# A graph layer on one core: 107 picked sets and 985 gathered chunks in place of 109 and 945, with the spare rows gathered a turn later

## The chip, the cores and the metric

The kernel runs on one core of a Trainium2 chip. A core has a matrix engine (PE), a vector engine (DVE), a scalar engine (ACT), a general engine (POOL, also called GpSimd), a queue engine (SP), and 16 DMA engines that move data between the chip's main memory and the core's own memory. Each engine works through its own list of instructions in order, and waits on semaphores where it needs another's result.

The metric is the device time of one execution in microseconds (us). The kernel before took 1822.46 us as the median of three runs (1816.8, 1824.37, 1822.46). One more execution was recorded by the profiler; it took 1817.15 us, and its span of instructions is 1815.4 us.

## The reference

```python
# x: (12500, 128) f32; src, dst: (400000,) int32, sorted by dst; edge_type: 0 or 1
Xs = X[src]
m_data = Xs @ W_data.T + b_data
m_ctrl = Xs @ W_control.T + b_control
msg = jnp.where((edge_types == 0)[:, None], m_data, m_ctrl)
agg = jax.ops.segment_sum(msg, dst, num_segments=X.shape[0])
out = jax.nn.relu(agg + (X @ W_self.T + b_self))
return layernorm(X + out)
```

For every edge the row of its source node is taken, sent through one of two matrices, and summed over the edges of each destination node. The kernel sums the rows of x by destination and type first, and multiplies by the matrices after that, 25 times for 500 nodes each.

## The kernel before

**Chunks, groups, sets.** The 400000 edges, sorted by destination, are 3125 chunks of 128 edges. 125 chunks are a group (25 groups, about 500 destination nodes each). A group is five stretches of 25 chunks, each of 5 chunks of one kind ("p", gathered) and 20 of the other ("e", picked). The rows of x of a chunk can reach PE in two ways:

- **Gathered**: one indirect DMA on POOL's queue reads the 128 rows of a chunk (three bf16 parts of each, 768 bytes, 96 KB in all) from a table in main memory into a tile `msg` (`fetch`, line 742). PE then sums them by destination with three matmuls and a fourth that counts (`gathered`, `chunk`, line 773), the columns chosen by a 0/1 matrix `psel` that DVE makes for five or 25 chunks at once.
- **Picked**: the 20 chunks of one stretch are a *set*. All of x lies in the core's memory as 98 blocks of 128 rows. The edges of a set are sorted into cells by block, at most 32 to a cell, and a 0/1 matrix `pick` lets PE pull their rows out of the blocks: 96 to 98 matmuls a set into `got`, copied by ACT into `emsg` (12 copies), then 75 matmuls with `esel`, and 25 that count. DVE makes `O`, `prod`, `rm`, `rv`, `pick` and `esel` for it, some 27 instructions. `there` and `pick` go through main memory on SP's queue (6.2 KB out, 800 KB back).

Some cells get more than 32 edges. What is too much, up to 64 rows of a set, are the **spare rows**: their list `idx` is made by PE and ACT (`spare_slots`, `keep`), and one more indirect DMA on POOL's queue reads them into a tile `last` (`spare_rows`, line 789). ACT fills the other half of `last` (`last_rows`, line 827, the copy at L831), and PE reads it with the last three matmuls of the set (`sums<-esel,last`).

**How many sets a group has.** `sets(g)` (line 176) gives 5 for every third group, else 4. Where it is 4, the last stretch of the group is gathered as a whole, 25 chunks (`of_p`, line 180). With g from 0 to 24, nine groups have five sets and 16 have four: 109 sets, and 945 gathered chunks.

**The order of the work.** The loop at line 1058 runs over the 109 sets. A set has six *turns* of four blocks (`unit(t)`, line 845, t from 0 to 5), and `merged` sorts what else is to be done between them: the gathered chunks, spread evenly over the sets from the third on; the making of the matrices for the sets to come; the preparation of the next group's codes; and, where a group's last chunk has passed, its finishing (`finish`, `pass_on`, `begin_acc`). The end of a set (`end`, line 877) is issued behind the first matmuls of the next one (`ending()` in turn 0). In it `keep_codes` also makes the `idx` of the next set on ACT.

**The order on POOL's queue.** `paced` (line 752) is called twice a turn. Each call issues at most one gather, and ties it to a matmul of that turn (`gate`), so that it can't start before. If a spare gather is asked for it goes first; else the next chunk's gather, if it is due: its due time is the place of the chunk 14 before it (`AHEAD`, line 1053). In the second call of an even turn only a chunk that was due two and a half turns earlier is taken. 18 tiles `msg` exist (`HOLD`). The spare gather is asked for in turn 1 (lines 847 and 848), and from turn 2 on the tile `last` stands for the last block (line 861 ff). In a steady set of nine chunks the gathers are thus issued in the turns 0, 1 (spare), 1, 2, 2 or 3, 3, 4, 5, 5 or the like.

Of the kernel before, what the change touches and what calls it, by code (L numbers as in the profile page):

```python
# [29 lines left out]
NE = 5  # L30
# [116 lines left out]
def evenly(units, a=0.0, b=1.0):  # L147
    return [(a + (b - a) * (k + 0.5) / len(units), u) for k, u in enumerate(units)]


def short_path(ctx, tc, const, ident, eps, wT, brow, bad, x, src, dst, etype, ws, bs, out):
# [12 lines left out]
    def side():  # L164

        return ps1.tile([P, 512], FP, name="side")
# [8 lines left out]

    def sets(g):

        return NE if g % 3 == 0 else NE - 1

    def of_p(g, i):  # L180

        return PL if sets(g) < NE and i == NE - 1 else PB
# [3 lines left out]

    rows_p = (NE - 1) * PB + PL
    each_e = [(g, i) for g in range(NG) for i in range(sets(g))]
    raw = {}
    starts = {k: [c for kind, _, c, _ in windows(0) if kind == k] for k in "pe"}  # L190
# [309 lines left out]
    def select(sel, col, code2):  # L500

        rows, n, width = sel.shape
        shape = [rows, n, width // 2, 2]
        nc.vector.tensor_tensor(  # L504
            sel.rearrange("p n (w t) -> p n w t", t=2),
            col[:rows].rearrange("p (o w t) -> p o w t", o=1, t=2).to_broadcast(shape),
            code2.rearrange("p n (o t) -> p n o t", o=1).to_broadcast(shape),
            op=OP.is_equal,
        )
        return sel  # L510
# [179 lines left out]
    def sums():  # L690
        return ps2.tile([P, 512], FP, name="sums")

    def cells_of(ps, width, k):
        return ps[:, k * 2 * width:(k + 1) * 2 * width]

    def add_rows(out, msg, sel, start, stop):
        for j in range(3):
            nc.tensor.matmul(  # L698
                out, msg[:, j * D:(j + 1) * D], sel, start=(start and j == 0), stop=stop, skip_group_check=True
            )  # L700
# [21 lines left out]
    def pass_on(g):  # L722

        assert parts_in[g] == NE + sets(g)
        if g + 1 < NG:
            begin_acc(g + 1)
            added.append(nc.vector.tensor_add(acc[g + 1][:, :, :lap], acc[g + 1][:, :, :lap], acc[g][:, :, GN:]))

    def accumulate(g, i, ps, wide, width):

        begin_acc(g)
        parts_in[g] = parts_in.get(g, 0) + 1
        with tc.issue_after(added[-2].ins) if len(added) > 1 else ExitStack():
            at = nc.vector.value_load(raw["place"][0:1, g, i:i + 1], min_val=0, max_val=R - WMAX)
        win = acc[g][:, :, bass.ds(at, width)]
        added.append(nc.vector.tensor_add(win, win, ps[:, :4 * wide].rearrange("p (a w) -> p a w", w=wide)[:, :, :width]))  # L736
# [15 lines left out]
    def paced(now, gate):  # L752

        if spare:
            gather = spare.pop()()
        elif to_fetch and due[len(due) - len(to_fetch)] <= now:
            gather = fetch()
        else:
            return
        tc.add_manual_dep(  # L760
            gather.ins, gate.ins.name,
            mybir.DependencyInfo(mybir.DependencyClass.Sync, mybir.DependencyReason.DATA), reason="paced",
        )
# [25 lines left out]
    def spare_rows(w):  # L789
        msg = slots[w]["last"] = two.tile([P, 3 * D], BF, name="last")  # L790
        return nc.gpsimd.indirect_dma_start(  # L791
            out=msg[:OVF, :], out_offset=None, in_=rows3[:, :],
            in_offset=bass.IndirectOffsetOnAxis(ap=slots[w]["idx"], axis=0),
        )

    def picked(w, tiled, ending, fin_used, before):

        g, i = each_e[w]  # L800
        s = {"sel": {}, "msg": {}}
        per, pair = 4, 2

        def choose(q0, n=8):

            sel = select(sp.tile([P, 9, 2 * EW], BF, name="esel")[:, :n], code_col, slots[w]["code"][:, q0:q0 + n])
            for k in range(n):
                s["sel"][q0 + k] = sel[:, k]

        def pick(ps, q, a0=0):  # L810
            for a in range(a0, 4):
                last = nc.tensor.matmul(  # L812
                    ps[CAP * a:CAP * (a + 1), :], slots[w]["pick"][:, a * NQ + q, :],
                    x3[:, 4 * q + a - a0].rearrange("p j d -> p (j d)"), start=True, stop=True, skip_group_check=True,
                )
            return last

        def rows(q):
            ps = psg.tile([P, pair, 512], FP, name="got")
            msg = two.tile([P, pair, 3 * D], BF, name="emsg", bufs=5)  # L820
            for k in range(pair):
                last = pick(ps[:, k, :3 * D], q + k)
                s["msg"][q + k] = msg[:, k, :]
            nc.scalar.copy(msg, ps[:, :, :3 * D])  # L824
            return last

        def last_rows():
            q = NQ - 1
            ps = psg.tile([P, pair, 512], FP, name="got")[:, 0] if fin_used else side()
            pick(ps[:, :3 * D], q, 2)  # L830
            nc.scalar.copy(s["msg"][q][OVF:, :], ps[OVF:, :3 * D])  # L831

        def count(q):
            if q == 0:
                s["ps"] = sums()
            nc.tensor.matmul(  # L836
                cells_of(s["ps"], EW, 1)[CAP * (q % 4):CAP * (q % 4 + 1), :], one_col[:, :CAP], s["sel"][q],
                start=(q < 4), stop=(q + 4 >= NQ), skip_group_check=True,
            )

        def add(q0, q1):
            for q in range(q0, q1):
                add_rows(cells_of(s["ps"], EW, 0), s["msg"].pop(q), s["sel"][q], False, q == NQ - 1)

        def unit(t):

            if t == 1 and w > 0:
                spare.append(lambda: spare_rows(w))
            for q in range(t * per, (t + 1) * per, pair):
                gate = rows(q)  # L850
            paced(w + (t + 1) / turns, gate)
            if t % 2:
                paced(w + (t + 1) / turns, gate)
            else:
                paced(w + (t - 1.5) / turns, gate)
            if t in (0, 1):
                choose(8 * t)
            if t == 0:
                ending()
            if t == 2:  # L860
                assert not spare
                s["msg"][NQ - 1] = slots[w]["last"]
            if t == 3:
                choose(16, 9)
            if t > 0:
                for q in range((t - 1) * per, t * per if t < turns - 1 else NQ):
                    count(q)
            if t == turns - 2:
                last_rows()
            if t == 1 and before:  # L870
                before()
            if t > 0:
                add((t - 1) * per, t * per)
            for u in tiled.get(t, []):
                u()

        def end():

            early, *more = tiled.get(turns, [lambda: None])
            early()  # L880
            add((turns - 1) * per, NQ)
            for u in more:
                u()
            accumulate(g, 2 * i + 1, s["ps"], EW, EW)

        turns = (NQ - 1) // per
        return evenly([lambda t=t: unit(t) for t in range(turns)]), end


# [165 lines left out]
    def ending():  # L1055
        pass

    for w in range(pairs):
        g, i = each_e[w]
# [181 lines left out]
```

## Time and profile before

| | |
|---|---|
| median of three runs | 1822.46 us (1816.8 to 1824.37) |
| the profiled execution | 1817.15 us, span 1815.4 us |
| TensorE clock granted | 0.995 of full speed |
| gathers on POOL | 945 of chunks, 109 of spare rows |
| set, from L831 to L831 | 15.92 us on the mean of 108 |
| main memory traffic | 236.28 MB read, 18.01 MB written |

How to read the lines of the profile. PE is the matmuls, PEld the loading of their weights beside them. A group of instructions is given as: line, engine, operation, written tile `<-` read tiles, shapes, `x` count, then busy us and mean ns of one, and behind the second bar the idle time of that engine just before them, with what ended most of it. A row of the timeline begins with the start and the duration in us, and has in brackets the idle time before it and what released it. A row of waits names who waited, for whom, the total in us, the number of times and the longest. "issue" is idle time in which the engine waited for nothing that the profile shows. A row of one tile's or one line's instructions gives the least, median and greatest duration in ns and the first and last start in us. A row of a window gives its start and end, its length, the busy time of the engine and (x) the number of instructions, the granted clock, the share of the DMA engines and GB/s.

### The profile page before, as it was taken

What the parts mean: (1) busy time and instruction counts of PE and PEld (TensorE: products, weight loads), DVE (VectorE), ACT (ScalarE), POOL (GpSimd) and SP (SyncE); (2) the same over time, 40 slices, a digit from 0 to 9 for tenths busy, and PEclk for the clock granted to TensorE, in tenths of its full rate; (3) what the DMA queues carried; (4) which work ended last, traced back from release to release, by engine and by line L of the source; (5) the groups of instructions that cost most, each with busy time, mean ns of one, the idle gap of its engine ahead of it and who ended that gap; (6) DMA issues with size and microseconds to landing.
All of it is one profiled execution on the core that took longest, in us unless ns stands there. A gap on an engine that the chain in (4) does not pass through costs nothing.

```text
span 1815.4 us, 72710 instructions
## 1 busy us (share of the span) xinstructions
PE 1637.4 (90%) x30253; PEld 1300.4 (72%) x30253; DVE 1600.0 (88%) x4050; ACT 1265.9 (70%) x2501; POOL 1328.1 (73%) x1071
## 2 busy tenths in 40 slices
PE   0589899998999999999999999999999999999997
PEld 0367677777777777777777777777777777777776
DVE  8889999998988998999898989898898988898883
ACT  4567667776777677676777767676776777777675
POOL 0387878887787778777776888778777777777772
PEclk9999999999999999999999999999999999999999
DMA  8744453554455453453545444544434444444431
GB/s 228 221 145 144 126 160 115 161 153 138 127 160 159 119 159 100 155 157 120 157 122 172 135 149 120 156 155 119 151 110 153 149 150 124 140 157 130 140 117 55
DMA packets 189216, 259.13 MB, mean 143 GB/s; under 512 B 86081, under 2 KB 154987, under 8 KB 185804
## 3 DMA queue, kind: packets, MB, share of 16 engines
q1 hardware_dynamic: 127402, 149.67, 25.3%
q0 software_dynamic: 48848, 98.32, 19.6%
q10 hardware_dynamic: 12626, 6.40, 1.3%
q8 instruction: 238, 3.90, 0.9%
q14 instruction: 102, 0.84, 0.1%
HBM read 236.28 MB, written 18.01 MB: 140 GB/s over the span
## 4 chain that ended last, share of the span: by engine, by line
PE 33%; DVE 23%; DMA 10%; ACT 4%; issue 3%; DVEq 1%; SPq 0%; ACTq 0%
PE sums L698 15%; PE got L812 10%; DMA pick<-there 8%; DVE esel L504 4%; PE side L942 2%; DVE pick L684 2%; ACT emsg L824 2%; DVE rv L630 2%; PE side L642 2%; DVE found L602 2%; DVE prod L571 2%; DMA there<-cell 1%; PE sums L836 1%; DVE rm L504 1%; ACT h L972 1%
## 5 line engine op out<-in xcount | busy, mean ns | idle before, releaser
L747 POOL DMA_INDIRECT msg<-rows,pidx x945 | 1191.0, 1260 | 320.7 <-issue 190.6
L824 ACT CAST emsg<-got 128x768 bf16<-128x768 f32 x1308 | 983.1, 802 | 259.7 <-PE got L812 246.7
L698 PE MATMUL sums<-esel,emsg 128*128 128x176 bf16 x7848 | 718.8, 241 | 0.0
L698 PEld LDWEIGHTS <-emsg 128*128 128x128 bf16 x7848 | 571.4, 98 | 110.1 <-issue 91.8
L812 PE MATMUL got<-x,pick 128*32 128x384 bf16 x10512 | 572.0, 330 | 35.0 <-ACT emsg L824 29.1
L812 PEld LDWEIGHTS <-pick 128*32 128x32 bf16 x10682 | 237.1, 96 | 152.7 <-issue 42.1
L504 DVE TENSOR_TENSOR esel<-code_col,code 128x1408 bf16<-128x1408 bf16 x327 | 297.6, 910 | 9.5 <-PE sums L698 6.8
L791 POOL DMA_INDIRECT last<-rows,idx x109 | 133.4, 1224 | 140.8 <-ACT emsg L824 119.7
L698 PE MATMUL sums<-psel,msg 128*128 128x48 bf16 x2835 | 186.7, 184 | 1.6 <-DVE psel L504 1.6
L836 PE MATMUL sums<-esel,one_col 128*32 128x176 bf16 x2725 | 156.3, 240 | 18.2 <-DVE esel L504 16.9
L684 DVE TENSOR_SCALAR pick<-pick,lane_f 128x3200 bf16<-128x3200 bf16 x109 | 115.0, 1055 | 51.5 <-DMA pick<-there 51.1
L698 PEld LDWEIGHTS <-msg 128*128 128x128 bf16 x2835 | 152.5, 97 | 2.4 <-issue 2.2
L783 PE MATMUL sums<-psel,one_col 128*128 128x48 bf16 x945 | 150.7, 183 | 0.0
L736 DVE TENSOR_TENSOR acc<-acc,sums 128x352 f32 (+2 forms) x234 | 100.6, 430 | 52.4 <-PE sums L698 44.6
L504 DVE TENSOR_TENSOR O<-cell_col,blk 128x2000 bf16<-128x2000 bf16 x109 | 129.9, 1191 | 6.5 <-PE side L642 2.4
L593 DVE TENSOR_TENSOR prod<-O,ahead 128x2000 bf16<-128x2000 bf16 x109 | 129.7, 1190 | 0.0
L836 PEld LDWEIGHTS <-one_col 128*32 128x32 bf16 x2725 | 80.4, 97 | 59.3 <-issue 24.9
L642 PE MATMUL side<-rv,O 128*128 128x64 bf16 x2180 | 85.9, 196 | 39.4 <-DVE rv L630 39.0
L642 PEld LDWEIGHTS <-O 128*128 128x128 bf16 x2180 | 78.9, 101 | 45.8 <-DVE rv L630 44.0
L624 ACT CAST bits_b<-bits 128x24 bf16<-128x24 int32 x109 | 23.2, 213 | 117.6 <-DVE bits L622 111.3
L783 PEld LDWEIGHTS <-one_col 128*128 128x128 bf16 x945 | 90.5, 96 | 0.0
L630 DVE TENSOR_TENSOR rv<-rm,vals 128x1280 bf16<-128x1280 bf16 x109 | 89.0, 816 | 0.0
(172 smaller groups left out, 1959.7 us busy)
## 6 DMA issues: line engine op xcount, KB each, us to landing
pick<-there SPq DMA_DIRECT2D x109, 800.0 KB
acc<-acc_start SPq DMA_DIRECT2D x23, 1280.0 KB
msg<-rows,pidx POOLq DMA_INDIRECT x945
rows<-x SPq DMA_DIRECT2D x6, 1344.0 KB
xs<-in_x_dram SPq DMA_DIRECT2D x99, 62.5 KB
out_dram<-h SPq DMA_DIRECT2D x99, 62.5 KB
xt<-in_x_dram ACTq DMA_DIRECT2D x6, 896.0 KB
there<-cell SPq DMA_DIRECT2D x109, 6.2 KB
```

The costliest lines, as they stand in the source:

```text
L504: nc.vector.tensor_tensor(sel.rearrange("p n (w t) -> p n w t", t=2), col[:rows].rearrange("p (o w t) -> p o w t", o=1, t=2).to_broadcast( ...
L593: nc.vector.tensor_tensor(prod, s["O"], ahead.rearrange("p (o j) -> p o j", o=1).to_broadcast([P, EC, NCELL]), op=OP.mult)
L630: nc.vector.tensor_tensor(rv.rearrange("p c v (r t) -> p c v r t", t=2), rm.rearrange("p c (o r t) -> p c o r t", o=1, t=2).to_broadcast(s ...
L642: nc.tensor.matmul(s["rk"][:m, :2 * CAP], s["held"][:, c * NCELL:c * NCELL + m], s["rv"][:, c].rearrange("p v r -> p (v r)"), start=(c == ...
L684: nc.vector.tensor_scalar(t, t, lane_f, None, op0=OP.is_equal)
L698: nc.tensor.matmul(out, msg[:, j * D:(j + 1) * D], sel, start=(start and j == 0), stop=stop, skip_group_check=True)
L747: return nc.gpsimd.indirect_dma_start(out=msg, out_offset=None, in_=rows3[:, :], in_offset=bass.IndirectOffsetOnAxis(ap=codes["p", g][0][: ...
L783: nc.tensor.matmul(cnt, one_col, sel, start=False, stop=(c == n - 1), skip_group_check=True)
L791: return nc.gpsimd.indirect_dma_start(out=msg[:OVF, :], out_offset=None, in_=rows3[:, :], in_offset=bass.IndirectOffsetOnAxis(ap=slots[w][ ...
L812: last = nc.tensor.matmul(ps[CAP * a:CAP * (a + 1), :], slots[w]["pick"][:, a * NQ + q, :], x3[:, 4 * q + a - a0].rearrange("p j d -> p (j ...
L824: nc.scalar.copy(msg, ps[:, :, :3 * D])
L836: nc.tensor.matmul(cells_of(s["ps"], EW, 1)[CAP * (q % 4):CAP * (q % 4 + 1), :], one_col[:, :CAP], s["sel"][q], start=(q < 4), stop=(q + 4 ...
```

## The change

Every fourth group, not every third, has five sets: g = 0, 4, 8, ... 24 are seven groups, the other 18 have four. That makes 107 sets, and 985 gathered chunks. The gather of the spare rows is asked for in turn 2 in place of turn 1, and the tile `last` is taken for the last block in turn 3 in place of turn 2.

```diff
     def sets(g):
 
-        return NE if g % 3 == 0 else NE - 1
+        return NE if g % 4 == 0 else NE - 1
...
         def unit(t):
 
-            if t == 1 and w > 0:
+            if t == 2 and w > 0:
                 spare.append(lambda: spare_rows(w))
             for q in range(t * per, (t + 1) * per, pair):
                 gate = rows(q)
...
-            if t == 2:
+            if t == 3:
                 assert not spare
                 s["msg"][NQ - 1] = slots[w]["last"]
```

The order of gathers in a steady set becomes: turns 0, 1, 1, 2 (spare), 3, 3, 4, 5, 5, with one more chunk in some turn 0, 2 or 4. The gathered chunks per set rise from 945 / 107 = 8.8 to 985 / 105 = 9.4, counted over the sets from the third on. Nothing else is edited; the last group has five sets in both.

## The prediction

> **What bounds the kernel now.** I read the engines' busy times first, then the groups of POOL (GpSimd), then POOL in order of time.
>
> ```profile
> span 1815.4 us, 72710 instructions
> PE 1637.4 (90%) x30253; PEld 1300.4 (72%) x30253; DVE 1600.0 (88%) x4050; ACT 1265.9 (70%) x2501; POOL 1328.1 (73%) x1071
> ```
>
> By this page PE and DVE are nearly full and POOL has a quarter of the span to spare. The groups by line and the waits of POOL correct that:
>
> ```profile
> L747 POOL DMA_INDIRECT msg<-rows,pidx x945 | 1191.0, 1260 | 320.7 <-issue 190.6 <-PE got L812 80.0 <-PE sums L698 14.0
> L791 POOL DMA_INDIRECT last<-rows,idx x109 | 133.4, 1224 | 140.8 <-ACT emsg L824 119.7 <-issue 10.4 <-ACT idx L541 10.2
> ...
> POOL msg L747 <- issue: 190.6, 619, 2.3
> POOL last L791 <- ACT emsg L824: 119.7, 71, 67.0
> POOL msg L747 <- PE got L812: 80.0, 162, 3.2
> ...
> 596.25 0.94 POOL L747 DMA_INDIRECT msg<-rows,pidx  x1 [0.30 <-issue]
> 597.97 0.94 POOL L747 DMA_INDIRECT msg<-rows,pidx  x1 [0.78 <-PE got L812]
> 600.74 0.90 POOL L791 DMA_INDIRECT last<-rows,idx  x1 [1.83 <-ACT emsg L824]
> 601.95 1.36 POOL L747 DMA_INDIRECT msg<-rows,pidx  x1 [0.30 <-issue]
> 603.61 1.43 POOL L747 DMA_INDIRECT msg<-rows,pidx  x1 [0.30 <-PE sums L698]
> 605.35 0.95 POOL L747 DMA_INDIRECT msg<-rows,pidx  x1 [0.30 <-issue]
> 606.60 1.63 POOL L747 DMA_INDIRECT msg<-rows,pidx  x1 [0.30 <-PE side L812]
> ```
>
> The timeline shows a gap of 0.30 us after nearly every gather, whatever it is put down to. In the waits, "issue" is 190.6 us over 619 times, again 0.31 each. So 0.305 us belongs to each of the 1054 gathers; only what exceeds it, as the 1.83 at 600.74, is real waiting.
>
> ```profile
> L747 POOL DMA_INDIRECT msg<-rows,pidx x945: 940/1105/5497, 74.0 to 1779.8; - x189
> L791 POOL DMA_INDIRECT last<-rows,idx x109: 897/1072/2382, 71.3 to 1789.4; - x109
> ```
>
> POOL's stretch thus runs from 71.3 to 1790 us. The sum: busy 1191.0 + 133.4 = 1324.4; idle 320.7 + 140.8 less the 67.0 before its very first gather = 394.5; together 1718.9 us. Of the idle, 1053 x 0.305 = 321 is the fixed gap, so POOL really waits 73 us, 4% of its stretch. It is almost a second bound: 1324.4 / 1054 = 1.257 us each, with the gap 1.562.
>
> What it does not do yet is hold PE up: the chunk matmuls, which read its messages, sit idle for 1.6 us in all, and that is for DVE.
>
> ```profile
> L698 PE MATMUL sums<-psel,msg 128*128 128x48 bf16 x2835 | 186.7, 184 | 1.6 <-DVE psel L504 1.6
> ```
>
> So today PE with DVE sets the pace, 1718.9 us of it beside POOL's stretch, and POOL follows 4% below. What lies outside that stretch, 1817.15 (the profiled execution's own time) - 1718.9 = 98.3 us, is the prologue, the last sets and the launch, and I carry it over unchanged.
>
> **The change part by part.** Sets fall from 9 x 5 + 16 x 4 = 109 to 7 x 5 + 18 x 4 = 107. Gathered chunks rise from 3125 - 109 x 20 = 945 to 3125 - 107 x 20 = 985. Gathers in the loop: 945 + 109 = 1054 becomes 985 + 107 = 1092.
>
> Two sets removed. The copies of L831 come once a set, so their starts measure it:
>
> ```profile
> 178.30 0.47 ACT L831 CAST last<-side 64x384 bf16<-64x384 f32 x1
> ...
> 222.84 0.47 ACT L831 CAST last<-side 64x384 bf16<-64x384 f32 x1
> ...
> L831 ACT CAST last<-side x85: 473/473/475, 80.4 to 1800.0; 64x384 bf16<-64x384 f32 x85
> ```
>
> Over the whole loop (1800.0 - 80.4) / 108 = 15.92 us, but that has the 25 groups' own work in it (finishing rows, preparing codes), which the change leaves at 25. The three sets from 178.30 to 222.84, in which no group is finished, take 14.85 each. Two of those are 29.7 us, with some 18 gathered chunks in them that are not saved but move to other sets. Every PE, ACT and DVE instruction of a set goes with it, its two SP transfers too.
>
> Forty chunks more. What one costs PE stands in its order of time:
>
> ```profile
> 603.13 0.24 PE L698 MATMUL sums<-psel,msg 128*128 128x48 bf16 x3
> 603.21 0.18 PE L783 MATMUL sums<-psel,one_col 128*128 128x48 bf16 x1
> 603.23 0.23 PE L698 MATMUL sums<-psel,msg 128*128 128x48 bf16 x3
> 603.31 0.18 PE L783 MATMUL sums<-psel,one_col 128*128 128x48 bf16 x1
> 603.42 0.83 PE L812 MATMUL got<-x,pick 128*32 128x384 bf16 x16
> ...
> 605.18 0.24 PE L698 MATMUL sums<-psel,msg 128*128 128x48 bf16 x3
> ...
> 605.37 0.83 PE L812 MATMUL got<-x,pick 128*32 128x384 bf16 x16
> ```
>
> The matmuls' own times overlap; from start to start a second chunk adds 0.10 us, a single one 0.19. I take 0.15. The net for PE is then -29.7 + (18 + 40) x 0.15 = -21 us, with bounds of -23.9 and -18.7. DVE's share of a chunk is 42.5 us of psel / 945 = 0.045, 2 us for forty, hidden in the same two sets. ACT does nothing for a chunk.
>
> ```profile
> L504 DVE TENSOR_TENSOR psel<-near_col,pcol 128x240 bf16<-128x240 bf16 (+1 forms) x125 | 42.5, 340 | 22.6 <-issue 22.3
> ```
>
> POOL's thirty-eight gathers more are the price. If each costs what one costs now, POOL needs 1092 x 1.562 = 1705 us. The other bound comes from why a gather takes 1.257 us when the shortest takes 0.94:
>
> ```profile
> 572.57 1.59 POOL L747 DMA_INDIRECT msg<-rows,pidx  x1 [0.30 <-issue]
> 574.47 0.95 POOL L747 DMA_INDIRECT msg<-rows,pidx  x1 [0.30 <-issue]
> ...
> 572.99 1.05 DVE L684 TENSOR_SCALAR pick<-pick,lane_f 128x3200 bf16<-128x3200 bf16 x1
> 573.96 0.17 DVE L608 SCALAR_TENSOR_TENSOR key<-rank,pk 128x20 f32<-128x20 bf16 x1
> ```
>
> The gather at 572.57 has DVE's 1.05 us comparison of pick inside it and ends just after that; the next has only small DVE work beside it and takes 0.95. The stretch above the minima is 1324.4 - 945 x 0.94 - 109 x 0.897 = 338 us, 3.1 per set. If it belongs to a set's long DVE work and not to the gathers, it falls with the sets: 985 x 0.94 + 107 x 0.897 + 107 x 3.1 + 1091 x 0.305 = 1687. I take 1698, slightly nearer the upper end, since more gathers in a set must also meet more of its DVE work. The Trainium skill ("SBUF — State Buffer", section "SBUF: two separate sides") says that GpSimd cannot write a gather's descriptors while VectorE runs in a mode that takes the shared port pair; the two rows agree, and by that rule alone the 1687 would stand.
>
> The spare rows a turn later. They now come second in a set's order of gathers, and behind two further gathers after the change: 2 x 1.56 = 3.1 us later when POOL is busy. What they need is early enough in both; what reads them comes at the set's end:
>
> ```profile
> 613.30 0.29 ACT L541 ACTIVATE idx<-part 64x1 int32<-64x1 f32 x1
> ...
> 615.24 0.90 POOL L791 DMA_INDIRECT last<-rows,idx  x1 [0.30 <-ACT emsg L824]
> ...
> 626.97 0.39 PE L698 MATMUL sums<-esel,last 128*128 128x176 bf16 x3
> ```
>
> Here from 616.1 to 627.0 is 10.8 us of cover, less the transfer. Moved back by 3.1 it still holds; if POOL is a set behind it is gone, and PE then waits in order with the whole next set queued behind it. The gain: of the 73 us that POOL waits, 119.7 - 67.0 - 70 x 0.305 = 31 us are the spare's, and with the idx a turn older most of that goes. Of the others, PE's gates at L812 are 80.0 - 162 x 0.305 = 31. POOL waits only when it has caught up, and at a full load it seldom has; between 0 and 31 I take 17.
>
> The transfers: 40 x 96 KB more through the gathers, 2 x 800 KB less for pick. They lie beside compute on the DMA engines, and cost nothing unless pick's landing becomes later.
>
> The sum. PE with DVE alone would now need 1718.9 - 21 = 1698 us of that stretch; POOL needs 1698 + 17 = 1715. POOL ends last: 98.3 + 1715 = 1813, against 1817.15 before, so **-4 us**. The median of the runs shown, 1822.46, stands 5.3 above the profiled execution; on its scale I forecast **1818**. Most of PE's gain is eaten because POOL becomes the bound.
>
> **The rivals.**
>
> A: POOL is never last, and PE's 21 us come through: 1796 by the profiled execution, 1801 on the median's scale. It needs POOL's mean with its gap below (1698 - 17) / 1092 = 1.54 us, that is a gather of 1.235. The 1687 above gives 1.545, so it's near. For it: every gather is some 14 chunks ahead of its use, 14 / (985 / 105) = 1.5 sets, and that buffer evens out short sets. Against it: the mean is 1.257 today.
>
> B, the other side: POOL runs slower at full load, and the spare rows, which have the least cover, come too late; PE stops at L698's sums<-esel,last once a set. Stretches in which POOL is never caught up show the price:
>
> ```profile
> 210.00:260.00 50.00, 40.26 (x32) 1.00 0.50 152
> 460.00:510.00 50.00, 40.01 (x32) 1.00 0.41 127
> ...
> sum 350.00, POOL 282.38; mean POOL 40.34
> ```
>
> Seven stretches of 50 us chosen for having no real wait, so 67.6 us of gaps / 0.305 = 222 gathers, 1.577 us each. If all ran so: 1092 x 1.577 = 1722, and 98.3 + 1722 + 17 = 1837, on the median's scale 1843, slower by 1.1%. It decides from 1.558 us on ((1718.9 - 17) / 1092). Against it: stretches chosen for no wait are those with long gathers by chance. For it: 1.558 is below today's 1.562.
>
> C: pick's landing, for which DVE already waits 51.1 us in 42 sets, gets later by the denser gathers and eats the gain: about no change, 1822.
>
> ```profile
> L684 DVE TENSOR_SCALAR pick<-pick,lane_f 128x3200 bf16<-128x3200 bf16 x109 | 115.0, 1055 | 51.5 <-DMA pick<-there 51.1
> ```
>
> **How the numbers follow.** The runs shown spread by 0.4%, so about 0.5% (9 us) can be told from no change. Forecast 0.33, A 0.33, B 0.31, C 0.03. Each per cent of the 1.562 us is 17 us, which is why three cases so far apart get like chances. The forecast's own range is 1805 to 1830; to hold 8 in 10 it must reach A and most of B: 1797 to 1846. The forecast lies mostly within 0.5%, a tail of it on the faster side; A is faster, B slower: 0.35, 0.34, 0.31.
>
> **What would show it.** Right: real waits of POOL (idle above 0.305 a gather) fall from 73 us to below 30, and PE's last or DVE's accumulate begin to name a late spare or message. Sets without a finish take longer than 14.85. A would show 1.235 us or less a gather and no such waits; B a mean above 1.26 and waits of tens of us at the sets' end. It would be wrong in another way if the loop lost less than 19 us of PE's work, or if waits on pick grew.

## The result and the profile after

The changed kernel takes 1843.16 us (median of five runs, 1838.65 to 1856.7), the kernel before 1818.0 us beside it (median of five, 1814.63 to 1824.37). The ratio is **1.0143, with a 95% interval of 1.0094 to 1.0191**: slower by 1.4%, where 0.2% faster was forecast. The profiled execution is the longest of the five, 1856.7 us; it is weighed below against another of 1842.96.

First the page of the changed kernel, its span and the engines' busy times:

```profile
span 1854.9 us, 71940 instructions
PE 1637.9 (88%) x29945; PEld 1295.2 (70%) x29945; DVE 1578.8 (85%) x3996; ACT 1249.6 (67%) x2463; POOL 1397.9 (75%) x1109
```

PE's share falls from 90 to 88%, DVE's from 88 to 85%; only POOL's rises. POOL's groups by line, in the form of before:

```profile
L747 POOL DMA_INDIRECT msg<-rows,pidx x985 | 1263.1, 1282 | 328.3 <-issue 203.3 <-PE got L812 69.6 <-DMA msg<-rows,pidx 11.9
L791 POOL DMA_INDIRECT last<-rows,idx x107 | 131.1, 1225 | 104.9 <-ACT emsg L824 82.0 <-issue 15.3 <-ACT cnt L920 5.2
```

Its waits, and then those of PE (who waited for whom, total, times, longest):

```profile
POOL last L791 <- ACT emsg L824: 82.0, 48, 67.5
POOL msg L747 <- PE got L812: 69.6, 137, 2.8
...
PE sums L698 <- DMA last<-rows,idx: 43.7, 15, 6.5
...
PE sums L698 <- DMA msg<-rows,pidx: 1.9, 3, 0.8
```

The sum of the prediction, made again: busy 1263.1 + 131.1 = 1394.2 us, 1.277 a gather. Idle 328.3 + 104.9 - 67.5 before the first = 365.7, of which 1091 x 0.305 = 333 is the fixed gap, so POOL really waits 33 us. Its stretch is 1760 us and 97 us lie outside it. Against before, 41 us longer: 70 more busy, 12 more gaps, 40 less waiting. The gathers did not become shorter, 1.277 us in place of 1.257. PE now stops at the set's end for the spare rows, 15 times; among its waits before, none is for `last`. From the first to the last copy of L831 the loop takes 1758.4 us in place of 1719.6, though it has two sets less.

One such stop, in order of time: POOL first, DVE beside it, then PE, and the granted clock of PE by windows (start and end, length, busy, clock, share of the DMA engines, GB/s):

```profile
192.94 2.96 POOL L747 DMA_INDIRECT msg<-rows,pidx  x1 [0.30 <-PE sums L698]
196.21 3.87 POOL L747 DMA_INDIRECT msg<-rows,pidx  x1 [0.30 <-issue]
200.38 0.94 POOL L747 DMA_INDIRECT msg<-rows,pidx  x1 [0.31 <-issue]
201.63 1.63 POOL L747 DMA_INDIRECT msg<-rows,pidx  x1 [0.30 <-issue]
203.56 1.11 POOL L791 DMA_INDIRECT last<-rows,idx  x1 [0.30 <-issue]
...
195.99 0.97 DVE L504 TENSOR_TENSOR esel<-code_col,code 128x1584 bf16<-128x1584 bf16 x1
196.88 0.48 DVE L504 TENSOR_TENSOR rm<-rank_col,rank 128x640 bf16<-128x640 bf16 x1
...
197.54 0.81 DVE L630 TENSOR_TENSOR rv<-rm,vals 128x1280 bf16<-128x1280 bf16 x1
...
198.37 0.86 DVE L504 TENSOR_TENSOR esel<-code_col,code 128x1408 bf16<-128x1408 bf16 x1
...
200.66 1.08 PE L698 MATMUL sums<-esel,emsg 128*128 128x176 bf16 x12
208.22 0.62 PE L698 MATMUL sums<-esel,last 128*128 128x176 bf16 x3 [6.49 <-DMA last<-rows,idx]
...
200.00:207.00 7.00, 1.74 (x32) 1.00 0.57 182
207.00:214.00 7.00, 5.78 (x71) 0.51 0.53 112
```

Two gathers of 2.96 and 3.87 us go ahead; beside the second DVE runs four long comparisons and products almost without a break. There is no real wait on POOL, only queueing. The spare gather starts at 203.56, when PE has stood for 1.8 us, and its rows reach PE 4.7 us later, at 208.2: 6.49 us in all. From 207.0 on, 1.2 us before PE goes on, it gets half its clock for 6.8 us (0.51 in the window), so a stop costs PE more than its length.

### The profile page after: what moved, and what is told of

Same layout as the page of the kernel before. It is cut to its first block, busy times and chain, and to the rows that moved or that the text cites. A ratio compares the mean times of both kernels' runs of the same rounds, so it can differ in the third digit from the quotient of the medians.

```text
span 1854.9 us, 71940 instructions
## 1 busy us (share of the span) xinstructions
PE 1637.9 (88%) x29945; PEld 1295.2 (70%) x29945; DVE 1578.8 (85%) x3996; ACT 1249.6 (67%) x2463; POOL 1397.9 (75%) x1109
## 3 DMA queue, kind: packets, MB, share of 16 engines
q8 instruction: 236, 3.87, 0.8%
## 4 chain that ended last, share of the span: by engine, by line
PE 33%; DVE 32%; DMA 18%; issue 8%; ACT 6%; POOL 2%; DVEq 1%; SPq 0%; ACTq 0%; POOLq 0%
PE sums L698 14%; DMA pick<-there 10%; PE got L812 9%; DVE esel L504 5%; ACT emsg L824 3%; PE side L942 3%; DVE pick L684 3%; DMA last<-rows,idx 3%; DVE rv L630 2%; DVE found L602 2%; DVE prod L571 2%; DMA there<-cell 2%; POOL msg L747 2%; DVE prod L593 1%; DMA msg<-rows,pidx 1%
## 5 line engine op out<-in xcount | busy, mean ns | idle before, releaser
L747 POOL DMA_INDIRECT msg<-rows,pidx x985 | 1263.1, 1282 | 328.3 <-issue 203.3
L824 ACT CAST emsg<-got 128x768 bf16<-128x768 f32 x1284 | 966.2, 803 | 280.7 <-PE got L812 265.2
L812 PEld LDWEIGHTS <-pick 128*32 128x32 bf16 x10486 | 231.1, 96 | 144.2 <-issue 34.6
L504 DVE TENSOR_TENSOR esel<-code_col,code 128x1408 bf16<-128x1408 bf16 x321 | 293.1, 913 | 8.1 <-PE sums L698 7.9
L791 POOL DMA_INDIRECT last<-rows,idx x107 | 131.1, 1225 | 104.9 <-ACT emsg L824 82.0
L698 PE MATMUL sums<-psel,msg 128*128 128x48 bf16 x2955 | 190.9, 184 | 9.9 <-DVE psel L504 7.9
L698 PEld LDWEIGHTS <-msg 128*128 128x128 bf16 x2955 | 156.8, 98 | 12.4 <-issue 9.1
L684 DVE TENSOR_SCALAR pick<-pick,lane_f 128x3200 bf16<-128x3200 bf16 x107 | 113.5, 1061 | 56.5 <-DMA pick<-there 55.8
L783 PE MATMUL sums<-psel,one_col 128*128 128x48 bf16 x985 | 155.0, 183 | 0.0
L589 DVE TENSOR_REDUCE ahead<-side 128x100 bf16<-128x500 f32 x107 | 72.3, 676 | 20.1 <-PE side L520 19.2
```

What stands on the lines that cost most here:

```text
L504: nc.vector.tensor_tensor(sel.rearrange("p n (w t) -> p n w t", t=2), col[:rows].rearrange("p (o w t) -> p o w t", o=1, t=2).to_broadcast( ...
L684: nc.vector.tensor_scalar(t, t, lane_f, None, op0=OP.is_equal)
L698: nc.tensor.matmul(out, msg[:, j * D:(j + 1) * D], sel, start=(start and j == 0), stop=stop, skip_group_check=True)
L747: return nc.gpsimd.indirect_dma_start(out=msg, out_offset=None, in_=rows3[:, :], in_offset=bass.IndirectOffsetOnAxis(ap=codes["p", g][0][: ...
L783: nc.tensor.matmul(cnt, one_col, sel, start=False, stop=(c == n - 1), skip_group_check=True)
L791: return nc.gpsimd.indirect_dma_start(out=msg[:OVF, :], out_offset=None, in_=rows3[:, :], in_offset=bass.IndirectOffsetOnAxis(ap=slots[w][ ...
```

## The experiments

The runs come in five batches, each with the kernel before beside it, and ratios are to that one. The batches are of two kinds, which has to be known to read them: in some the kernel before takes some 1820 us, in others 2060. What is known of the difference is in the last section; I call them quick and slow batches. The expectations, written beforehand, speak of chips in their place.

**The two edits apart (quick batch, kernel before 1830.08 us).** The counts alone:

```diff
-        return NE if g % 3 == 0 else NE - 1
+        return NE if g % 4 == 0 else NE - 1
```

> The changed counts of sets (107 sets, 985 gathered chunks) with the spare rows gathered in turn 1 as before. Theory R (POOL has become the bound: 1092 gathers at about 1.58 us each with the gap, wherever the spare stands in the order): 1830 to 1850 us, within 10 us of the changed kernel. Theory S (the spare rows a turn later are what made PE wait, and the counts alone gain): about 1800 us, and PE's waits on the tile last gone.

The turn alone is the rest of the change with `g % 3` kept.

> The counts of before (109 sets, 945 gathered chunks), the spare rows gathered in turn 2. R: 1815 to 1825 us, no change that can be told, since POOL still has some 70 us of real waiting. S: 1835 us or more, with PE waiting on the tile last as in the changed kernel.

Measured: 1838.56 us, ratio 1.003 (1.0005 to 1.0056), for the counts; 1838.43, ratio 1.0031 (1.0000 to 1.0061), for the turn. The turn alone costs next to nothing, as theory R had it. The counts gain nothing, against S. But R's "within 10 us of the changed kernel" could only be judged in one batch with it, so the counts and the changed kernel were run again below.

**POOL's load alone, taken off and put on (same batch).** Taken off the changed kernel: every eighth chunk's gather is left out, and its matmuls read the message of the chunk before.

```diff
+    n_out, held = [0], [None]
...
-        msg = mp.tile([P, 3 * D], BF, name="msg")
+        n_out[0] += 1
+        if n_out[0] % 8 == 0:
+            fetched.append(held[0])
+            return None
+        msg = held[0] = mp.tile([P, 3 * D], BF, name="msg")
...
+            return
+        if gather is None:
             return
```

> The changed kernel with the gather of every eighth chunk left out (123 of 985); that chunk's matmuls read the message of the chunk before. PE, DVE and ACT do the same work. R: POOL needs 969 x 1.58 = 1530 us and is never last, so what is left is the time of PE with DVE, 1796 us by the prediction's term of -21 us; PE's waits on last and msg gone. S: the spare rows are still asked for a turn late, so most of the 25 us of loss stays: above 1825 us.

Put on the kernel before: 37 gathers that nobody reads.

```diff
         fetched.append(msg)
+        if len(to_fetch) % 25 == 24:
+            nc.gpsimd.indirect_dma_start(
+                out=mp.tile([P, 3 * D], BF, name="msg"), out_offset=None, in_=rows3[:, :],
+                in_offset=bass.IndirectOffsetOnAxis(ap=codes["p", g][0][:, at:at + 1], axis=0),
+            )
```

> The kernel before with 37 gathers more, spread evenly, whose rows nobody reads (each takes one of the 18 message tiles for a moment). The work of the other engines and the place of the spare are unchanged. R: 1091 gathers at 1.57 us are as long as POOL's whole stretch before, so PE begins to wait: 1830 to 1850 us. S: within 0.5% of 1818 us.

Measured: 1810.5 us, ratio 0.9894 (0.9851 to 0.9937), with gathers left out; 1836.02, ratio 1.0042 (1.0016 to 1.0069), with 37 more. POOL's groups of these two. Their lines are moved down, L747 and L791 to L752 and L798 in the first, to L752 and L796 in the second; the gathers that nobody reads are at L748:

```profile
L752 POOL DMA_INDIRECT msg<-rows,pidx x862 | 1093.7, 1269 | 404.8 <-PE got L819 206.0 <-issue 166.3 <-PE side L520 9.1
L798 POOL DMA_INDIRECT last<-rows,idx x107 | 146.4, 1368 | 133.0 <-ACT emsg L831 111.6 <-issue 8.9 <-ACT cnt L927 6.9
```

```profile
L752 POOL DMA_INDIRECT msg<-rows,pidx x945 | 1165.1, 1233 | 310.5 <-issue 189.0 <-PE got L817 66.4 <-PE sums L698 14.0
L796 POOL DMA_INDIRECT last<-rows,idx x109 | 135.8, 1246 | 134.5 <-DMA bias<-b_parts 68.7 <-ACT emsg L829 42.3 <-issue 12.5
L748 POOL DMA_INDIRECT msg<-rows,pidx x37 | 44.4, 1200 | 11.3 <-issue 10.1 <-PE got L817 0.9 <-DMA msg<-rows,pidx 0.3
```

With an eighth of the gathers gone POOL waits for PE's gates (206.0 us at L819), and the loss turns into a gain of 1.1%: the loss hangs on the gathers. With 37 more the kernel before loses 0.4%, and not the 0.7 to 1.7% that R expected. PE does not begin to wait: its waits on gathered rows are 0.5 us in that profile, and POOL still really waits 55 us (310.5 + 134.5 + 11.3 - 68.7 - 1090 x 0.305). So this run does not show POOL as the bound, nor that time goes with the number of gathers alone; the turn alone, with 1054 gathers, took 1838.43 us, as long as the counts alone with 1092. What costs these three kernels 0.3 to 0.4% each in this batch is open; DVE's wait on pick's landing is 58 to 70 us in them, 51.1 before.

**All of it in one batch (quick, kernel before 1823.49 us).** The changed kernel, the counts alone, the changed kernel with the spare rows one turn later still, and the kernel before with every eighth gather left out:

```diff
-            if t == 2 and w > 0:
+            if t == 3 and w > 0:
...
-            if t == 3:
+            if t == 4:
                 assert not spare
```

> The changed kernel beside the next three on one chip. Theory H (at a full POOL queue the spare rows come too late for the set's end, and PE's wait there stops the loop): about 1.010 to 1.014 of the kernel before, PE's wait on the tile last some 40 us, and clearly above the run with the counts alone. Theory R (only the number of gathers counts): equal to the run with the counts alone.

> The counts alone, the spare rows in turn 1. H: about 1.003 of the kernel before, with no wait on last, PE waiting some 20 us for chunk messages instead. R: the same as the changed kernel beside it.

> The changed kernel with the spare rows asked for one turn later still, in turn 3. H: two more gathers go ahead of them, 3 us later at every set's end, so PE's wait on last at least doubles and the ratio rises by a further 0.01 or more. R: unchanged against the changed kernel, since the number of gathers is the same.

> The kernel before with every eighth chunk's gather left out, as before, on another chip if it falls so. If it gets the 0.95 again, gathers cost the other engines time even where POOL waits. If the chip is like that of the first runs: 0.99 to 1.00, since POOL then only follows PE.

| run | median us | ratio, 95% interval |
|---|---|---|
| changed kernel | 1842.26 | 1.0110 (1.0067 to 1.0152) |
| counts alone, spare in turn 1 | 1838.02 | 1.0096 (1.0070 to 1.0123) |
| spare in turn 3 | 1861.9 | 1.0204 (1.0168 to 1.0239) |
| before, an eighth left out | 1813.63 | 0.9957 (0.9937 to 0.9976) |

For each, POOL's groups and PE's waits on gathered rows. The changed kernel:

```profile
L747 POOL DMA_INDIRECT msg<-rows,pidx x985 | 1244.8, 1264 | 326.7 <-issue 198.3 <-PE got L812 72.5 <-PE sums L698 9.4
L791 POOL DMA_INDIRECT last<-rows,idx x107 | 137.4, 1285 | 105.1 <-ACT emsg L824 80.5 <-issue 18.0 <-ACT cnt L920 3.9
...
PE sums L698 <- DMA last<-rows,idx: 37.0, 12, 6.0
```

The counts alone:

```profile
L747 POOL DMA_INDIRECT msg<-rows,pidx x985 | 1242.1, 1261 | 312.0 <-issue 197.2 <-PE got L812 56.0 <-DMA msg<-rows,pidx 18.0
L791 POOL DMA_INDIRECT last<-rows,idx x107 | 141.1, 1319 | 106.6 <-DVE pcode L444 67.4 <-ACT emsg L824 20.7 <-issue 12.5
...
PE sums L698 <- DMA msg<-rows,pidx: 28.2, 29, 2.3
```

The spare in turn 3:

```profile
L747 POOL DMA_INDIRECT msg<-rows,pidx x985 | 1249.7, 1269 | 330.0 <-issue 208.8 <-PE got L812 76.3 <-PE sums L698 12.5
L791 POOL DMA_INDIRECT last<-rows,idx x107 | 138.7, 1296 | 122.7 <-ACT emsg L824 100.0 <-issue 17.9 <-ACT cell L650 1.5
...
PE sums L698 <- DMA last<-rows,idx: 59.0, 26, 6.1
```

The three have POOL busy for 1382, 1383 and 1388 us, nearly the same, and differ in its real waits: 31, 18 and 52 us, by the same sum as above. Their profiled times, 1842.96, 1832.45 and 1867.73 us, follow those. So both theories have a part. The counts alone cost 1.0%, most of the 1.1%. The place of the spare decides where PE stops: for messages in turn 1 (28.2 us), for `last` in turn 2 (37.0). Between turns 1 and 2 the times can't be told apart, which R expected and H did not; between 2 and 3 the step is 0.9%, about as H expected, though the wait on `last` grew only from 37 to 59 us and did not double. POOL's real waits grew by 21 us in that step, 17 of them before the spare gathers themselves (105.1 - 67.6 - 106 x 0.305 = 5 us, then 122.7 - 67.8 - 106 x 0.305 = 23), behind which the chunk gathers of the queue wait too.

The same kernel, the counts alone, has the ratios 1.0030 and 1.0096 in two batches whose intervals don't meet. Between batches, some 0.7% of such a ratio isn't the kernel's.

All quick profiles side by side: the mean length of a gather, POOL's real waits (by the sum above), and what the gathers have in the chain of work that ended last, which the profile follows back from the last instruction. For that last column POOL's own time and the landing of `msg` and `last` are added; the chain can be followed over 1340 us of the kernel before, and over 1713 to 1847 us of the others.

| kernel | gathers | sets | mean gather, us | real waits, us | in the chain, us |
|---|---|---|---|---|---|
| before | 1054 | 109 | 1.257 | 73 | 2.5 |
| the turn alone | 1054 | 109 | 1.274 | 78 | 14 |
| before, 37 more | 1091 | 109 | 1.233 | 55 | 7 |
| before, an eighth left out | 936 | 109 | 1.268 | 243 | 16 |
| the counts alone, two profiles | 1092 | 107 | 1.270, 1.267 | 23, 18 | 129, 143 |
| changed kernel, two profiles | 1092 | 107 | 1.277, 1.266 | 33, 31 | 117, 120 |
| spare in turn 3 | 1092 | 107 | 1.271 | 52 | 154 |
| changed, an eighth left out | 969 | 107 | 1.280 | 174 | 31 |

Gathers hold up the loop where 1092 of them meet 107 sets, and little elsewhere (31 us at most); 1091 of them beside 109 sets do not. Their mean length follows neither their number nor how much POOL waits.

**The slow batches (kernel before 2060.64, 2063.23 and 2062.35 us in the three).** The next runs were to settle the same questions and came out slow. The first of these batches:

> The changed kernel once more, beside the kernel before and the next three on one chip, since the kernel before took 1818 us in its first runs and 1830 us beside the last four. If the two edits interact (spares with less cover at a full POOL queue), the ratio stays near 1.014 while each edit alone gave 1.003. If the 1.014 was partly the chip or the hour, it falls to 1.006 or less, the sum of the two.

> The kernel before once more, for a profile on the same chip. Theory R says that a slower chip or hour shows as longer gathers: a mean above 1.257 us where the time is above 1817 us. Ratio 1.000.

> The kernel before with the gather of every eighth chunk left out (118 of 945); that chunk's matmuls read the message of the chunk before. If PE with DVE sets the pace before the change and POOL only follows, as the prediction had it, the ratio is 1.00. If POOL already holds the kernel before in stretches, it is 0.99 or below. Against the run with every eighth left out of the changed kernel (0.9894) it gives the worth of two sets less and forty chunks more for PE alone: the prediction says 21 us, 1.15%.

> Every eighth group has five sets: 104 sets, 1045 gathered chunks, 1149 gathers, the spare rows in turn 1. R: 57 gathers more than the run with the counts alone (1838.56 us), at 1.575 us each: 90 us longer, about 1925 us. If instead the time followed the number of sets (PE), it would be some 30 us shorter than that run.

Measured: changed kernel 2100.39 us, ratio 1.0178 (1.0143 to 1.0213); the kernel before 2063.1, 1.0006; before with an eighth left out 1960.26, 0.9525 (0.9491 to 0.9559); every eighth group with five sets 2167.04, 1.0532 (1.0487 to 1.0578). More gathers cost time here too, and fewer sets bring none, but R's reason fails. A slower batch does not show longer gathers, and POOL is no bound:

```profile
L747 POOL DMA_INDIRECT msg<-rows,pidx x945 | 1177.9, 1246 | 509.7 <-PE got L812 248.6 <-issue 173.8 <-PE sums L698 32.4
L791 POOL DMA_INDIRECT last<-rows,idx x109 | 111.6, 1024 | 232.1 <-ACT emsg L824 111.0 <-DMA bias<-b_parts 68.1 <-ACT idx L541 44.2
```

This is the kernel before in it. A gather takes 1.223 us ((1177.9 + 111.6) / 1054), less than the 1.257 of the quick profile, and POOL waits 353 us (idle as above, 674, less 1053 x 0.305). Yet 118 gathers less bring 100 us, 0.85 each.

**What two sets are worth to PE, and what stretches a gather (slow again).** The two kernels with every eighth gather left out, and the changed kernel with one DVE operation cut to a sliver. In the one, `pick` keeps raw lane numbers:

```diff
-        return [(0.6, lambda: half(0, NCELL))]
+        return [(0.6, lambda: half(0, 1))]
```

In the other the product of 2000 elements a row shrinks to 100, and the halving after it reads `O`, so the ranks are left out:

```diff
-                prod, s["O"], ahead.rearrange("p (o j) -> p o j", o=1).to_broadcast([P, EC, NCELL]), op=OP.mult
+                prod[:, :1], s["O"][:, :1], ahead.rearrange("p (o j) -> p o j", o=1).to_broadcast([P, 1, NCELL]), op=OP.mult
...
-            nc.vector.tensor_add(half, prod[:, :, :h], prod[:, :, h:])
+            nc.vector.tensor_add(half, s["O"][:, :, :h], s["O"][:, :, h:])
```

> The changed kernel with the gather of every eighth chunk left out (that chunk's matmuls read the message before), beside the same of the kernel before. By the term of -21 us it lies 1.15% below that one; if two sets less are worth less to PE and DVE than 14.85 us each, 0.6% or less.

> The kernel before with the gather of every eighth chunk left out. 0.995 to 1.00 of the kernel before, as in the last run, and 1.15% above the run beside it if the term of -21 us was right.

> The changed kernel with DVE's comparison that makes pick (L684) cut from 3200 to 32 elements a row, so that the rest of pick keeps the raw lane numbers: about 107 us of DVE work less, of the kind with one source. If DVE's work stretches the gathers, their mean falls from 1.27 us by what they met of it, some 0.04 us, and with POOL as the bound the time falls by 1092 x 0.04 = 44 us, to 0.985 of the kernel before or below. If it does not, the mean stays at 1.27 and the time at 1.01.

> The changed kernel with DVE's product prod<-O,ahead (L593) cut from 2000 to 100 elements a row, and the halving after it reading O in its place, so that ranks and what follows from them are not the reference's: about 120 us of DVE work less, of the kind with two sources. By the shared port as the Trainium skill has it (SBUF - State Buffer), work with two sources stops only GpSimd's reads, so the mean gather would fall less than in the run beside it. If all long DVE work stretches gathers alike, it falls by 0.04 us or more here too.

Measured: the eighth left out, changed kernel 1996.25 us, 0.9681 (0.9660 to 0.9702), kernel before 1964.24, 0.9515 (0.9487 to 0.9542), where 0.995 to 1.00 was expected. Here two sets less and forty chunks more do not gain but lose 1.6%, which is 0.97 us for each of the 33 gathers between them. The cut comparison: 2080.15, 1.0104 (1.0052 to 1.0156); the cut product: 2118.19, 1.0274 (1.0217 to 1.0331). POOL's gathers and the operation that was cut: the changed kernel in the first slow batch, the cut comparison, and the cut product:

```profile
L747 POOL DMA_INDIRECT msg<-rows,pidx x985 | 1200.6, 1219 | 600.4 <-PE got L812 345.6 <-issue 188.1 <-remote 33.7
L791 POOL DMA_INDIRECT last<-rows,idx x107 | 142.0, 1327 | 127.7 <-DMA bias<-b_parts 67.4 <-ACT emsg L824 27.2 <-issue 21.0
L684 DVE TENSOR_SCALAR pick<-pick,lane_f 128x3200 bf16<-128x3200 bf16 x107 | 112.8, 1054 | 30.6 <-DMA pick<-there 27.5 <-issue 2.8
L593 DVE TENSOR_TENSOR prod<-O,ahead 128x2000 bf16<-128x2000 bf16 x107 | 127.4, 1190 | 0.0
```

```profile
L747 POOL DMA_INDIRECT msg<-rows,pidx x985 | 1162.1, 1180 | 640.9 <-PE got L812 381.1 <-issue 182.5 <-remote 32.4
L791 POOL DMA_INDIRECT last<-rows,idx x107 | 120.4, 1125 | 128.5 <-DMA bias<-b_parts 68.3 <-ACT emsg L824 27.3 <-issue 23.8
L684 DVE TENSOR_SCALAR pick<-pick,lane_f 128x32 bf16<-128x32 bf16 x107 | 25.4, 238 | 32.6 <-DMA pick<-there 27.8 <-issue 3.8
```

```profile
L747 POOL DMA_INDIRECT msg<-rows,pidx x985 | 1097.2, 1114 | 660.6 <-PE got L812 389.7 <-issue 171.2 <-remote 51.7
L791 POOL DMA_INDIRECT last<-rows,idx x107 | 142.1, 1328 | 191.6 <-ACT emsg L824 96.0 <-DMA b_parts<-part 64.2 <-ACT xT L931 14.1
L593 DVE TENSOR_TENSOR prod<-O,ahead 128x100 bf16<-128x100 bf16 x107 | 21.6, 202 | 0.0
```

DVE's long work does stretch gathers: 87 us less of the comparison (112.8 to 25.4) takes 60 us off the chunk and spare gathers together (1342.6 to 1282.5), 106 us less of the product (127.4 to 21.6) takes 103 off (to 1239.3). The second run of the cut product, below, has 1248.5 us of gathers, so such totals repeat within some 10 us. In these batches it brings no time, because POOL waits anyway; that the cut product is slower (1.0274) than the changed kernel in the other batch (1.0178) isn't explained. The last two runs:

> Every second group has five sets: 113 sets, 865 gathered chunks, 978 gathers, the spare rows in turn 1. Where POOL is near its bound (a chip on which the kernel before takes some 1820 us): POOL falls out of the way and PE pays for four sets, by the two runs with every eighth gather left out 0.3% a set (0.9957 at 109 sets, 0.9894 at 107): 0.9957 + 0.0126 = 1.008. Where hand-overs are slow (2060 us): each gather less was worth 0.85 us (100 us for 118), so 76 gathers less bring 65 us and the ratio is about 0.97 to 0.98.

> The changed kernel with the product cut to 100 elements a row, once more. On a chip of some 1820 us: the mean gather falls from 1.27 to about 1.17 us (it fell by 0.095 on the other), POOL's need by 104 us, so POOL is never last and the time is that of PE with DVE, 0.985 of the kernel before or below. On a chip of some 2060 us: 1.027 again.

They came out slow too (kernel before 2062.35 us). Every second group with five sets takes 2019.58 us, ratio **0.9782** (0.9756 to 0.9808), as expected for this case, the fastest kernel of the slow batches that computes the whole; its price in a quick batch was not measured. The cut product gave 1.0299 (1.0262 to 1.0336). So whether less DVE work would free POOL's bound, and bring time, in a quick batch stays open.

## Why the prediction was wrong

**That POOL becomes the bound was right.** It was the forecast's own case. The gathers have 117 and 120 us of the chain that ended last in the two profiles of the changed kernel, 2.5 us before, and without every eighth of them the loss is gone (0.9894). The fixed gap of 0.305 us holds too. The run with 37 idle gathers is no proof of it: beside 109 sets POOL kept 55 us of real waiting.

**The step that failed is the price of the 1092 gathers.** I put it at 1698 us, "slightly nearer the upper end" of 1687 to 1705. It measured 1394 + 333 = 1727 in the first profile and 1382 + 333 = 1715 in the other: above both ends. The lower end took the stretch over the least length for a property of the sets, so that fewer sets would give shorter gathers. But at 107 sets that stretch, by the prediction's own sum, is 372 us (3.5 a set) in the first profile and 360 (3.4) in the other, and 334 (3.1) where 123 gathers are left out, so it is no property of the sets. The upper end took the mean of one profile, 1.257 us, for what a gather costs. Over the ten quick profiles it lies between 1.233 and 1.280. With the gap, 1092 gathers cost 1679 to 1731 us by that, and the price from which POOL decides, 1.558 us, lies inside (1.538 to 1.585). What moves the mean is open: with 37 gathers more at 109 sets the stretch was even less, 324 us for 338. That DVE's long work stretches gathers is shown; that a POOL which seldom waits meets more of it is not, since the longest mean, 1.280, stands where POOL waits 174 us.

**POOL's real waits** were the second term that was too small: put at 17 us, they came out at 33 and 31. I let the spare's share go and halved the gates'. The spare's share went (82.0 - 67.5 - 47 x 0.305 = 0 us, from 31); the gates' stayed (69.6 - 137 x 0.305 = 28 us, from 31), for a reason that no run shows. In the counts alone all real waits together are 18 us, near my figure.

**The spare rows' cover.** "If POOL is a set behind it is gone": it was gone 15 times in the first profile and 12 times in the other. That it would be dear in the step from turn 1 to turn 2 is not shown: 1.0096 and 1.0110 can't be told apart, and alone the turn gave 1.003. From turn 2 to 3 it costs 0.9%.

**PE's gain of 21 us** is not confirmed. With POOL out of the way the ratios were 0.9894 at 107 sets and 0.9957 at 109, some 11 us apart, in different batches, and batches differ by as much; in the slow batches the sign is the other. How much two sets are worth in a quick batch stays open.

**The rivals.** B had the right sign, and its price of 1.577 us a gather came near the 1.582 and 1.571 measured. That its 1843 us on the median's scale meets the measured 1843.16 is luck: its waits were 17 us in place of 33, PE stopped for `last` 15 times and not once a set, and a gather took 1.585 us also where POOL waited 174 us, so stretches without a wait are not what made it dear. A did not come, and needed 1.54 us a gather. C did not come in the changed kernel: DVE's wait on pick's landing is 55.8 us in 42 sets in the first profile and 50.8 in 45 in the other, 51.1 before. In the counts alone it is 69.9 and 59.9. The choice between ends 18 us apart decided the sign, at 17 us for each per cent of a gather's length.

## What to carry to other kernels

An engine that is "73% busy" may be full: look in the order of time for a gap that follows every instruction, add it to the price, and count only what exceeds it as slack. When an edit moves work to an engine that is already within 5% of its limit, one profile's mean is too coarse a price: here it moved by 0.9% between two profiles of the changed kernel and by 4% over all ten, and 1% of it decided the sign. Take the price from several profiles, and where the sign of the sum changes within their range, forecast no sign. A queue in which something with a deadline stands behind things without one wants that deadline checked at full load. A ratio of 1% found in one batch may be 0.3% in the next, so compare variants in one batch.

## What the runs showed that was not expected

**Two kinds of batch.** In the slow batches the hand-over from PE to ACT takes longer. ACT's copies of `got` in the kernel before, slow and then quick (in brackets the idle time before):

```profile
701.27 1.55 ACT L824 CAST emsg<-got 128x768 bf16<-128x768 f32 x2 [1.61 <-PE got L812]
703.70 1.50 ACT L824 CAST emsg<-got 128x768 bf16<-128x768 f32 x2 [0.87 <-PE got L812]
```

```profile
601.92 1.50 ACT L824 CAST emsg<-got 128x768 bf16<-128x768 f32 x2 [0.71 <-PE got L812]
603.98 1.50 ACT L824 CAST emsg<-got 128x768 bf16<-128x768 f32 x2 [0.56 <-PE got L812]
```

Take the copies for which ACT already stood idle when the last of their matmuls ended (the ends of matmuls are modelled in the profile, alike in both). In the quick profile these are 400, and the copy starts 0.08 us after that end on the mean, at most 0.11. In the slow one they are 237, with 0.63 us on the mean and up to 3.5. It is the matmul's signal that comes late: the semaphore is updated 0.04 us after the end in the one, 0.54 in the other, on the mean. In the slow profile it goes with the gathers: 0.84 us where a gather was running when the matmul ended (142 copies), 0.32 where none was, and 0.11 where none ran at any moment in between (67); in the quick one it is 0.08 and 0.09 with and without. That gathers cause it is argued from this and from the 0.85 us that each one less brought.

What makes a batch slow is open. The chip's number on record is 13 and 9 for the quick batches and 0, 5 and 13 for the slow batches. So 13 stands with both kinds, an hour apart, and whether that was the same chip is not known.

**Work with two sources stretches gathers at least as much as work with one.** By the runs above, each microsecond less of the comparison, which has one source, shortened the gathers by 0.69 us (60 / 87); each one less of the product, which has two, by 0.98 (103 / 106). The Trainium skill ("SBUF — State Buffer", section "SBUF: two separate sides") has work of one source in the modes with two ports lock GpSimd out, and work with two sources only against GpSimd work that reads that memory. The gathers here behave as if the second were at least as strong. The two operations stand at different places in a set's work, so that the number of sources makes the difference is not shown.

**A stop of PE has an echo.** In the first profile of the changed kernel 16 stretches have half the granted clock, 80 us in all, against five, 22 us, before. But for the last, at the end, each begins between 3.0 us before and 1.6 us after the moment where PE takes up work again after 1.96 us or more without; two stops of 2.3 and 2.4 us have none. The whole span's clock falls from 0.995 to 0.979.
